# A decoder on one core: the first place in the self attention's work memory, and how that memory is handed over

## The chip, the core and the metric

The kernel runs on one core of a Trainium2 chip. The metric is device time in microseconds (us) for one execution, as a median over runs. The engines are PE (TensorE; PEld is its weight load), DVE (VectorE), ACT (ScalarE), POOL (GpSimd) and SP (SyncE, which issues DMA transfers).

## What is computed

Two decoder layers on `x` of 8 x 256 tokens, 512 wide, all in float32. Each of the six steps adds its result to `x` and normalises:

```python
x = _layernorm(x + _L0_attn_ref(x, ...))    # differential attention
x = _layernorm(x + _L0_xattn_ref(x, ...))   # long convolution
x = _layernorm(x + _L0_ffn_ref(x, ...))     # experts, 2 of 8 for each token
x = _layernorm(x + _L1_attn_ref(x, ...))    # causal self attention, 16 heads of 32
x = _layernorm(x + _L1_xattn_ref(x, ...))   # cross attention
x = _layernorm(x + _L1_ffn_ref(x, ...))     # attention with one routed head of keys and values
```

The change concerns the border between the third step and the fourth, which is

```python
qkv = jnp.einsum('bsd,ed->bse', x, w_qkv).reshape(b, s, 3, H, HD).transpose(2, 0, 3, 1, 4)
q, k, v = qkv[0], qkv[1], qkv[2]
scores = jnp.einsum('bhqd,bhkd->bhqk', q, k) * HD ** (-0.5)
scores = jnp.where(causal, jnp.float32(-1000000000.0), scores)
a = jax.nn.softmax(scores, axis=-1)
ctx = jnp.einsum('bhqk,bhkd->bhqd', a, v).transpose(0, 2, 1, 3).reshape(b, s, d)
return jnp.einsum('bsd,ed->bse', ctx, w_o)
```

## The kernel before

The 2048 tokens are 16 tiles of 128 (`x[0]` to `x[15]`), in four groups of four tiles (`TPG`, `NG`).

**The experts** end in `blocks`. For each block of 128 rows PE makes the result `po_m` (L1164), ACT or DVE copies it to a tile `y_m` (L124, L126), and SP writes that tile to `ys` in DRAM (L1176). These tiles lie in the pool `m_work`. Behind the last block every engine reads a count and branches over spare blocks (L1256, L1263). The first four token tiles are already gathered and normalised during the last blocks, into a part of the weights' tile (the trace calls it `w_l1a`); the other twelve are gathered from `ys` during the self attention, by DMAs that POOL issues (L1279), and added up on DVE (L1287).

**The self attention** is one of three uses of `causal_attention` (L1316): `"a"` is the differential attention, `"s"` the self attention, `"r"` the routed one. It opens a pool of work memory, `{name}_work` (L1337), and pools for PSUM. Then it makes `neg`, `terms` and `take` in the work pool, and goes through units, each a set of four heads of one batch of 256 tokens:

- `maxima` (L1370): scores on PE (`ps_q`, L1378), copied by ACT to `rows` (L1387), masked on POOL (L1389), maxima on DVE (L1398);
- `weights` (L1430): transposed scores on PE (`ps_k`, L1441, L1450), exponentials on ACT (`pT`, L1458), mask and sums on POOL (L1459, L1469);
- `products` (L1471): values and sums on PE (`ps_pv`, L1484, L1495), reciprocal on DVE (L1503).

Projections run between them, in pieces with due times that `fill` and `need` hand out; the order of PE, DVE, ACT and POOL is fixed as it is written (`manual_schedule`). For a group, `prepare` (L1698) makes `qT`, `kT` and `v`, and calls `turned_batches` (L246). That returns steps which turn the tokens, so that the features lie on the partitions: four transposes on PE for each tile (L236) and one copy by ACT into `xT` (L237). One `xT` tile holds one batch, that is two token tiles, and is made when its first step runs; there are three buffers of it. The first projections are `feature_block` (PE `ps_f`, L212, copied by ACT at L1663) for `qT` and `kT`; each reads a whole `xT`. The values are `token_block` (PE `ps_t`, copied by ACT into `v_s`, L1712).

**How memory goes from one pool to the next.** When a pool ends, its bytes are free for the pools opened after it. With `reuse_waits="tile"` the first instruction that writes a tile waits for the instructions and DMAs that used what lay in that tile's own bytes. Without it, the first writes wait for all that used the freed bytes of the pool. Before the change only the work pool of `"r"` has this argument among the three; the pools of the experts that end here (`m_dn`, `m_work`) and the PSUM pools have it too.

Of the kernel before, what the change touches and what calls it, by code (L numbers as in the profile page):

```python
# [17 lines left out]
F32 = mybir.dt.float32  # L18
# [6 lines left out]
P = 128  # L25
B, S, D = 8, 256, 512
# [4 lines left out]
KB = D // P  # L31
# [24 lines left out]
def decoder_kernel(ctx: ExitStack, tc: tile.TileContext, a: dict, out: bass.AP):  # L56
# [175 lines left out]
    def turned(pools, dst, src, tag="mm"):  # L232

        pt = pools.tile([P, KB, P], F32, tag=tag, name="pt")
        for k in range(KB):
            nc.tensor.transpose(pt[:, k, :], src[:, k * P : (k + 1) * P], ident)  # L236
        nc.scalar.copy(dst, pt)  # L237

    class Batches(list):

        def __getitem__(self, at):
            rows, k, tokens = at
            b = tokens.start // S
            return list.__getitem__(self, b)[rows, k, tokens.start - b * S : tokens.stop - b * S]

    def turned_batches(work, pools, g):  # L246

        xT = Batches()

        def step(ti):  # L250
            if ti % 2 == 0:
                xT.append(work.tile([P, KB, S], F32, tag="xT", name="xT", bufs=3))
            dst = list.__getitem__(xT, ti // 2)
            turned(pools, dst[:, :, ti % 2 * P : (ti % 2 + 1) * P], x[g * TPG + ti])

        return [xT], [(0, [(TR, lambda ti=ti: step(ti))]) for ti in range(TPG)]
# [39 lines left out]
    def diff_attention(xh, ch):  # L296
# [213 lines left out]
        def finish(work, pools, t0, yT, at):  # L510
# [71 lines left out]
            return cost  # L582

        causal_attention("a", prepare, finish, 8, gather)
        st0.close()

# [729 lines left out]
    def causal_attention(name, prepare, finish, upb=KB, gather=None):  # L1316
# [17 lines left out]
        }  # L1334
        with ExitStack() as st:
            work = st.enter_context(
                tc.tile_pool(name=f"{name}_work", bufs=2, **({"reuse_waits": "tile"} if name == "r" else {}))  # L1337
            )
            ps_sc = st.enter_context(tc.tile_pool(name=f"{name}_sc", bufs=1, space=PSUM, reuse_waits="tile"))
            ps_pv = st.enter_context(tc.tile_pool(name=f"{name}_pv", bufs=1, space=PSUM, reuse_waits="tile"))  # L1340
# [9 lines left out]

            neg, terms = [], []
            for i in range(2):
                neg.append(work.tile([P, 3, 4, upb], F32, tag=f"neg{i}", name="neg", bufs=1))
# [333 lines left out]
    def self_attention(w, wqkv, homes, arrive):  # L1689
# [8 lines left out]
        def prepare(work, pools, g, at, here):  # L1698
            qT = work.tile([P, KB, GT], F32, tag="qT", name="qT")
            kT = work.tile([P, KB, GT], F32, tag="kT", name="kT")  # L1700
            v = work.tile([P, TPG, D], F32, tag="v", name="v_s")
            xT, turns = turned_batches(work, pools, g)

            def arriving(t, slot, place):
# [47 lines left out]
        def finish(work, pools, t0, yT, at):  # L1752
# [3 lines left out]
            return 2 * KB * MM  # L1756

        causal_attention("s", prepare, finish)


# [204 lines left out]
    def routed_attention(wqkv, wg):  # L1965
# [347 lines left out]
        def finish(work, pools, t0, yT, at):  # L2313
# [10 lines left out]
            return 2 * TR  # L2324

        causal_attention("r", prepare, finish)

    masks, clear_slots, load_experts, load_gu_last, router, blocks, combine, wide = experts(rt)
# [114 lines left out]
```

## Time and profile before

| | |
|---|---|
| median of the runs | 2052.21 us (2049.88 to 2056.38, 3 runs) |
| profiled execution | 2062.48 us, its span 2060.7 us |
| mean granted TensorE clock | 0.983 of full speed |
| experts, last blocks (1000 to 1050 us) | PE busy 50.00 us of 50.00 |
| border (1074 to 1080 us) | PE busy 3.46 us of 6.00, granted clock 0.81 |
| self attention (1120 to 1200 us) | PE busy 79.51 us of 80.00 |
| self attention (1200 to 1300 us) | PE busy 97.25 us of 100.00 |
| routed attention, end (1990 to 2040 us) | PE busy 35.50 us of 50.00, DVE 41.68, clock 0.83 |

All times in a profile count from the start of its span. In a row such as `PE L212 MATMUL ps_f<-xT,w_l1a`, the engine is followed by the source line, the operation and "written tile <- read tiles"; line numbers are those of the kernel before. `PEq`, `ACTq` and the like are the engine's own instruction queue, as apart from its data path. A matmul's end is modelled, so its busy time is approximate.

### The profile page before, as it was taken

The numbers are of one execution on the slowest core, as the hardware profiler recorded it, in microseconds if no ns is written. First come the engines' busy times: TensorE is split into PE (matmuls) and PEld (weight loads), VectorE is DVE, ScalarE is ACT, GpSimd is POOL, SyncE is SP. The second block draws the span as 40 slices with busy tenths as digits, with TensorE's granted clock in tenths as the row PEclk, the third lists the DMA queues.
The fourth block names the chain that finished last, engine by engine and source line by source line (L and its number), as shares of the span: only waits on it lengthen the run. The fifth ranks groups of instructions, "written<-read, shape, count | busy, mean of one in ns | idle before, by whom it ended". The sixth has DMA issues, their size and how long they took to land. (4 is left out here: it accounts for less than half of the span.)

```text
span 2060.7 us, 46451 instructions
## 1 busy us (share of the span) xinstructions
PE 1921.8 (93%) x20142; PEld 1141.9 (55%) x20142; DVE 1253.7 (61%) x1933; ACT 620.1 (30%) x793; POOL 858.0 (42%) x952
## 2 busy tenths in 40 slices
PE   8979999889998998999999999998999999988885
PEld 5545555444443445666555555544888887454443
DVE  4677878758888976122234757456344544437987
ACT  4555555520010003211114434432101011245552
POOL 3687777846556823000014645333100010216763
PEclk9999999989999999999999999999999999999997
DMA  6899953315115125213232212002101000260000
GB/s 230 311 386 380 383 168 84 94 52 212 31 46 184 52 98 188 77 65 129 80 110 84 84 34 83 2 2 81 49 16 41 21 21 1 90 191 15 25 24 32
DMA packets 138044, 219.24 MB, mean 106 GB/s; under 512 B 27440, under 2 KB 52144, under 8 KB 137840
## 3 DMA queue, kind: packets, MB, share of 16 engines
q1 hardware_dynamic: 131376, 195.93, 27.9%
q0 software_dynamic: 6464, 20.32, 2.9%
q8 instruction: 161, 2.64, 0.5%
q14 instruction: 43, 0.35, 0.1%
HBM read 104.42 MB, written 123.34 MB: 111 GB/s over the span
## 5 line engine op out<-in xcount | busy, mean ns | idle before, releaser
L1503 DVE RECIPROCAL rsum<-ps_pv 128x256 f32<-128x256 f32 x128 | 224.5, 1754 | 215.6 <-PE ps_pv L1495 215.4
L182 PE MATMUL ps_y<-kv,wt 128*128 128x512 f32 x640 | 280.0, 596 | 5.2 <-POOL kv L625 2.7
L1398 DVE TENSOR_REDUCE neg<-rows 128x12 f32<-128x1536 f32 x128 | 223.0, 1742 | 53.3 <-POOL rows L1389 53.2
L1458 ACT ACTIVATE pT<-ps_k 128x1536 f32<-128x1536 f32 x128 | 185.7, 1451 | 225.4 <-PE ps_k L1450 218.4
L1459 POOL TENSOR_SCALAR_AFFINE_SELECT pT<-pT 128x1024 f32<-128x1024 f32 x128 | 141.3, 1104 | 217.4 <-ACT pT L1458 217.2
L1387 ACT COPY rows<-ps_q 128x1536 f32<-128x1536 f32 x128 | 184.2, 1439 | 151.0 <-PE ps_q L1378 96.0
L1389 POOL TENSOR_SCALAR_AFFINE_SELECT rows<-rows 128x1024 f32<-128x1024 f32 x128 | 142.3, 1112 | 183.8 <-ACT rows L1387 183.1
L182 PEld LDWEIGHTS ps_y<-kv,wt 128*128 128x128 f32 x640 | 120.8, 191 | 156.3 <-issue 137.7
L1469 POOL TENSOR_TENSOR pT<-pT 128x512 f32<-128x512 f32 x112 | 147.1, 1313 | 9.3
L212 PE MATMUL ps_f<-xT,w_l1a 128*32 128x256 f32 x2048 | 123.4, 385 | 5.5 <-ACT xT L237 4.1
L1164 PE MATMUL po_m<-dn,hT 128*128 (+1 forms) x216 | 100.8, 603 | 4.0 <-issue 2.3
L148 POOL TENSOR_SCALAR rstd<-bn_mv 128x1 f32<-128x1 f32 x80 | 15.8, 198 | 212.5 <-DVE bn_mv L156 206.4
L1143 DVE TENSOR_TENSOR h_b<-h_b,pg 128x352 f32<-128x352 f32 x36 | 18.6, 516 | 124.0 <-ACT h_b L1142 124.0
L1495 PE MATMUL ps_pv<-pT,ones_v 128*32 128x256 f32 (+1 forms) x1152 | 87.1, 381 | 5.2 <-POOL pT L1469 5.1
L212 PEld LDWEIGHTS ps_f<-xT,w_l1a 128*32 128x32 f32 x2048 | 62.9, 111 | 51.2 <-issue 9.0
L663 DVE TENSOR_REDUCE yc<-z 128x64 f32<-128x512 f32 x128 | 86.1, 673 | 5.7 <-issue 5.2
L1279 POOL DMA_INDIRECT y<-ys,slots x4 | 4.0, 1007 | 204.4 <-PE pu L182 203.8
L1378 PEld LDWEIGHTS ps_q<-kT,qT 32*128 32x128 f32 x1536 | 49.5, 188 | 50.5 <-issue 18.1
L182 PE MATMUL pg<-gu,xT_b 128*128 x216 | 72.1, 470 | 3.6 <-ACT xT_b L237 3.6
L1378 PEld LDWEIGHTS ps_q<-kz,qT 32*128 32x128 f32 x1536 | 49.2, 188 | 47.2 <-ACT pT L1458 33.7
L1378 PE MATMUL ps_q<-kz,qT 32*128 32x128 f32 x1536 | 61.5, 289 | 14.3 <-ACT pT L1458 11.6
L1378 PE MATMUL ps_q<-kT,qT 32*128 32x128 f32 x1536 | 61.9, 290 | 12.7 <-ACT pT L1458 8.7
(411 smaller groups left out, 3694.2 us busy)
## 6 DMA issues: line engine op xcount, KB each, us to landing
xs<-zero SPq DMA_DIRECT2D x8, 4352.0 KB
ys<-zero SPq DMA_DIRECT2D x8, 4352.0 KB
filters<-in_L_xattn_k SPq DMA_DIRECT2D x4, 2560.0 KB
first_h<-xs SPq DMA_DIRECT2D x36, 256.0 KB
ys<-y_m SPq DMA_DIRECT2D x36, 256.0 KB
gu<-in_L_ffn_gate_up_proj SPq DMA_DIRECT2D x3, 2816.0 KB
wt<-filters SPq DMA_DIRECT2D x32, 256.0 KB
sorted_x<-zero SPq DMA_DIRECT2D x1, 5120.0 KB
```

The source lines that it names most:

```text
L182: nc.tensor.matmul(ps, lhsT=lhsT(k), rhs=rhs(k), start=(k == 0), stop=(k == n - 1))
L212: nc.tensor.matmul(ps[cs], lhsT=lhsT[:, cs], rhs=rhs, start=start, stop=stop)
L1164: nc.tensor.matmul(po, lhsT=hT[:m, i, :], rhs=dn[i][:m, bass.ds(e, 1), :], start=(i == 0), stop=(i == len(FCH) - 1),)
L1378: nc.tensor.matmul(block[:, s, j, :], lhsT=q(rows, c, b * S + i * P, P), rhs=k(rows, c, b * S + keys * P, P), start=True, stop=True,)
L1387: nc.scalar.copy(d.rearrange("p j s k -> p s j k"), block)
L1389: nc.gpsimd.affine_select(out=rows, in_=rows, compare_op=ALU.is_ge, fill=-FAR, base=0, pattern=[[0, 8], [-1, P]], channel_multiplier=1,)
L1398: return lambda: nc.vector.tensor_reduce(neg[u // upb % 2][:, :, :, c], d, AX.X, ALU.max, negate=True)
L1458: nc.scalar.activation(p[:, 0:3].rearrange("p j s q -> p s j q"), block, AF.Exp)
L1459: nc.gpsimd.affine_select(out=p[:, 0:2].rearrange("p j s q -> p (j s) q"), in_=p[:, 0:2].rearrange("p j s q -> p (j s) q"), compare_op=ALU ...
L1469: nc.gpsimd.tensor_tensor(p[:, 3], p[:, 1], p[:, 2], ALU.add)
L1495: nc.tensor.matmul(ps[32 * s : 32 * s + 32, 1, j * P :], lhsT=ones_v, rhs=p[:, 1, s, :] if j else first[:, :, s, :], start=(j == 0), stop= ...
L1503: nc.vector.reciprocal(r, ps[:, 1, :])
```

## The change

Three edits:

- In `causal_attention("s", ...)` the first tile made in the work pool is now an `xT` tile, made ahead of `neg`, `terms` and `take`, and left in a list `placed`.
- `turned_batches` takes that tile for its first batch, and makes its own for all later ones.
- The work pools of `"s"` and `"r"` are both handed over with `reuse_waits="tile"`; before, only that of `"r"` was.

```diff
+    placed = []
+
     def turned_batches(work, pools, g):
...
             if ti % 2 == 0:
-                xT.append(work.tile([P, KB, S], F32, tag="xT", name="xT", bufs=3))
+                xT.append(
+                    placed.pop()
+                    if placed
+                    else work.tile([P, KB, S], F32, tag="xT", name="xT", bufs=3)
+                )
...
-                tc.tile_pool(name=f"{name}_work", bufs=2, **({"reuse_waits": "tile"} if name == "r" else {}))
+                tc.tile_pool(name=f"{name}_work", bufs=2, **({} if name == "a" else {"reuse_waits": "tile"}))
...
+            if name == "s":
+                placed.append(work.tile([P, KB, S], F32, tag="xT", name="xT", bufs=3))
             neg, terms = [], []
```

In the built program the instructions of each engine stand in the same order before and after. What differs are the conditions some of them wait for:

| instruction (line before) | conditions before | after |
|---|---|---|
| ACT, first copy into `xT` (L237) | PE, 14 DMA counters, DVE, POOL, ACT | PE |
| PE, first `ps_f` (L212) | ACT, 15 DMA counters, DVE | ACT |
| DVE, `terms` (L1357) | PE, ACT, DVE, 6 DMA counters | an earlier PE instruction |
| POOL, first `rows` (L1389) | ACT, 8 DMA counters, DVE | ACT, 1 earlier DMA |
| POOL, four of the gathers (L1279) | data, earlier gathers | 1 or 2 DMA counters more |
| ACT, first `kT` (L1663) | PE | PE, earlier ACT and DVE instructions |
| PE, first `ps_q` (L1378) | ACT | ACT, DVE |
| ACT, first `v_s` (L1712) | PE | PE, 10 DMA counters |
| ACT, one `pT` (L1458) | PE | PE, 1 DMA counter |
| DVE, one `less` (L1412) | DVE | DVE, an earlier PE instruction |
| ACT, one copy in the cross attention (L1819) | PE, DVE | PE, DVE, 2 DMA counters |

## The prediction

> **What bounds the kernel now.** I read the page first: the span, the busy shares, and the granted clock.
>
> ```profile
> span 2060.7 us, 46451 instructions
> PE 1921.8 (93%) x20142; PEld 1141.9 (55%) x20142; DVE 1253.7 (61%) x1933; ACT 620.1 (30%) x793; POOL 858.0 (42%) x952
> PEclk9999999989999999999999999999999999999997
> ```
>
> PE is busy for 93% of the span, so there are few places where a wait can be taken out. Only one of them concerns this change: the start of the self attention. The chain of work that ended last, in order of time, shows it (start, length, what):
>
> ```profile
> 1074.11 2.00 DMA ys<-y_m
> 1076.11 0.02 issue
> 1076.13 0.04 ACTq L237
> 1076.17 0.04 issue
> 1076.21 1.08 ACT xT L237 x2
> 1077.30 0.04 issue
> 1077.34 5.39 PE ps_f L212 x64
> ```
>
> The last rows of the experts are written to DRAM, and only when that write has landed does ACT copy the first turned tokens; PE's first projection waits for the copy. The copies read the transposes and nothing of that write. Then the timeline (start, length, engine, line, operation, and in brackets the idle time before it with what ended it); the last line is a later stretch for comparison:
>
> ```profile
> 1073.50 0.59 ACT L124 COPY y_m<-po_m 128x512 f32<-128x512 f32 x1 [2.98 <-PE po_m L1164]
> 1073.72 1.08 PE L236 MATMUL pt<-ident,w_l1a 128*128 128x128 f32 x8 [0.30 <-PEq L1263]
> ...
> 1077.34 5.35 PE L212 MATMUL ps_f<-xT,w_l1a 128*32 128x256 f32 x64 [2.54 <-ACT xT L237]
> ...
> 1192.68 4.09 PE L212 MATMUL ps_f<-xT,w_l1a 128*32 128x256 f32 x72
> ```
>
> The transposes were done at 1074.80, and PE then stood idle for 2.54 us. What follows is slow too: 64 matmuls in 5.35 us, where 72 of the same kind later take 4.09 (64 by that rate: 3.64). Busy time by stretch tells why (stretch, length, PE, PEld, DVE, ACT, POOL busy with their instructions, granted clock, DMA share, GB/s):
>
> ```profile
> 1074.30:1077.71 3.41, 0.87 (x13) 0.55 (x15) 0.33 (x3) 1.07 (x2) 0.00 (x0) 1.00 0.35 129
> 1077.71:1081.13 3.42, 3.42 (x40) 1.70 (x33) 0.00 (x0) 0.38 (x1) 0.00 (x0) 0.50 1.01 379
> ...
> 1753.55:1756.97 3.42, 3.42 (x28) 2.86 (x27) 2.28 (x8) 2.33 (x5) 0.80 (x3) 1.00 0.00 0
> ...
> 1797.93:1801.34 3.41, 1.78 (x33) 1.17 (x34) 0.87 (x2) 0.58 (x1) 2.34 (x3) 1.00 0.85 308
> 1801.34:1804.75 3.41, 3.41 (x22) 1.28 (x17) 0.00 (x0) 1.44 (x1) 0.17 (x1) 0.50 0.34 105
> 1893.50:1896.91 3.41, 1.81 (x40) 1.18 (x40) 3.38 (x5) 2.34 (x2) 2.09 (x2) 1.00 0.00 0
> 1896.91:1900.33 3.42, 2.96 (x52) 1.32 (x56) 3.21 (x8) 1.44 (x2) 2.20 (x4) 1.00 0.23 81
> ```
>
> Every change of the granted clock lies on one grid of 3.41 us. A stretch of that grid in which PE is busy 0.87 or 1.78 us is followed by one at clock 0.50; after 1.81 us the clock stays at 1.00. So the wait costs twice: once as idle time, and once as a half-speed stretch behind it, in which PE was busy throughout.
>
> **The change part by part.** In the built program the order of instructions on all five engines is unchanged and no DMA is added or moved. Only waits differ, so the parts are waits.
>
> *The first copies and the first projection.* ACT's copy of xT loses 17 wait conditions and keeps the one on PE; PE's first `ps_f` loses 16 and keeps the one on ACT. When can the copies start? ACT ends its last `y_m` copy at 1073.50 + 0.59 = 1074.09 and the branch behind it by 1074.2 (ACT's own queue at L1263). Tile 0's four transposes end between 1073.72 + 0.54 (half of the eight) and 1073.72 + 0.66 (a lone group of four at 1095.59 takes 0.66). I take 1074.4 as the start, a little above both. The two copies together take 1.08, as in the chain, and tile 1's transposes, done at 1074.80, are there before the second copy wants them. End 1075.48; with 0.04 to PE (the chain's "issue") and a little for a semaphore, `ps_f` starts at 1075.55 and not at 1077.34: 1.8 us. Bounds: a start at 1074.26 gives 1077.34 − 1075.38 = 1.96; a start only after all eight transposes (1074.80 + 0.13) gives 1077.34 − 1076.05 = 1.29.
>
> *The half-speed stretch.* PE's idle time before `ps_f` becomes 0.30 + (1075.55 − 1074.80) = 1.05 us. However the grid falls, a stretch of 3.41 us then holds at least 2.36 us of PE work, well over the 1.81 after which the clock stayed up. The half-speed stretch therefore goes, and with it half of 3.41 = 1.71 us (by the rates above: 5.35 − 3.64 = 1.71, the same). Bounds: 0, if that stretch is not on this run's grid or stays for a reason not seen, and 1.71. I take 1.71, because it stands in the row.
>
> [...]
>
> *The waits that appear elsewhere.* The places of the tiles are new, so waits come up where a tile now lies on old bytes. ACT's first copy of `v_s` gets ten DMA conditions. They are among those that `xT` had, and all were met at 1076.11; the value projection (`ps_t`) that feeds this copy starts at 1102.96 in the chain. Queued behind that copy on ACT is `rows` L1387, for which POOL, then DVE, then PE would wait; the cover is some 27 us before and 23 after, so nothing. The first gathers on POOL get two writes to `ys` to wait for; they ran at 1093.60, and about 1090 after, 14 us behind the landing; behind them stands POOL's next `rows` select. `kT`, the first `ps_q`, `terms`, `less`, the first POOL `rows`, one `pT` and `u2` of the cross attention get one to three conditions each, on instructions that ended by 1076. Extra conditions cost 0.02 to 0.05 us each on a queue (the queue rows of L1263); ten of them before `v_s` are at most 0.5 us on ACT, which stands idle for 2 to 3 us around there. I put all of it at 0, bounds 0 and 0.5.
>
> *Does the gain reach the end?* After 1077 the waits list of all engines names DMA as the releaser of DVE's L1287 (4.9 us in total, gathers that POOL issues in step with the units), and of L2146 and L2158 (5.0 us, rows sorted on the chip just before). All are started by earlier work, so they move along. From 1080 to 1425 PE is busy in 95 to 99% of the time. What was PE's chain stays PE's chain, 3.5 us earlier.
>
> Sum: −1.8 − 1.71 + 0 = −3.5 us. The profiled execution took 2062.48 us (span 2060.7 and 1.8 around it), which becomes 2059.0 with a span of 2057.2. The median of the runs is 2052.21, 10.3 below the profiled one, so the gain is carried over as microseconds: 2048.7.
>
> **The rivals.**
>
> [...]
>
> *C: the change does not do what it says,* or another wait takes the place: the copies still end at about 1077. For it: the last write still takes its 2.00 us, and ten conditions of it still stand in ACT's queue. Against it: they stand 18 instructions later, at `v_s`. 2052.2.
>
> *D: slower, by the clock grid.* All later work moves against the grid. In the profile, seven stretches after 1082 had PE busy 52 to 58% and stayed at full clock (1893.50 is one; the others begin at 1429.29, 1432.70, 1941.29, 1992.49, 2006.14 and 2040.27). If only the wait goes, they move by 1.8 us, half a grid step, and may fall under. Each one that tips costs up to 1.71; from two (3.4) on, this eats the gain of 1.8. With four: 4 × 1.71 − 1.8 = +5.0: 2057.2. For it: unchanged runs lie between 2049.88 and 2056.38, nearly four such steps apart. Against it: the full gain of 3.5 is one whole grid step (3.41), so the later work comes to lie nearly as before; and after 1985 the chain runs through DVE for long parts, where PE's clock costs less.
>
> *E: the same, in the other direction:* two half-speed stretches fewer later on (the trace has them at 1801, 1835, 1999, 2020 and 2027): 3.5 + 3.4 = 6.9 less, 2045.3.
>
> **How the numbers follow.** Forecast A (2048.7) 0.50, B 0.14, C 0.12, D 0.10, E 0.14. A measurement of this kernel can tell about 0.3% from no change, 6.2 us: under 2046.0 is faster, over 2058.4 slower. The runs before lie from 2.3 below their median to 4.2 above it, and a median of a few runs moves by 2 to 3. So a quarter of A's weight (0.13) may come out under 2046, and E all of it: faster 0.27. Slower is D's upper part and what I have not seen, 0.08. Same 0.65. For the range, A with that scatter is 2046 to 2052; to leave out no more than 2 in 10 it takes in C and the nearer parts of D and E: 2043.5 to 2055.
>
> **What would show it.** Right: the chain at the start of the self attention has no `ys<-y_m` in it any more; ACT's two `xT` copies start near 1074.4 and no longer behind a DMA; PE's idle time before the first `ps_f` is about 0.8 us; 64 `ps_f` take 3.6 to 3.7 us and the clock there is 1.00; the first `ps_q` starts about 3.5 us earlier, and that distance still stands at the end of the self attention. Wrong: `ps_f` starts early but still takes over 5 us (B); a wait on a DMA in front of `v_s`, the gathers or `rows` (C); the distance shrinks in the last 250 us with more stretches at 0.50 (D).

## The result, and the profile after

| | before | after |
|---|---|---|
| median of 21 runs each, us | 2052.21 (2047.49 to 2056.95) | 2047.24 (2042.50 to 2052.47) |
| ratio after / before | | 0.998, 95% interval 0.9972 to 0.9989 |
| profiled execution, its span, us | 2060.7 | 2045.5 |

In this comparison the changed kernel is 0.2% faster: 5.0 us by the medians, 4.1 (2.3 to 5.7) by the ratio. That is less than the 0.3% at which the prediction began to call it faster. Two later comparisons of the same two kernels (medians of before 2059.43 and 2058.56 us) gave 0.9994 (0.9980 to 1.0008) and 0.9995 (0.9981 to 1.0009), neither of them clear of no change by itself. The three, weighted by the width of their intervals, give about 0.9986 (0.9980 to 0.9993), 2.8 us.

The page of the profile after begins so:

```profile
span 2045.5 us, 46438 instructions
PE 1915.1 (94%) x20142; PEld 1139.1 (56%) x20142; DVE 1253.4 (61%) x1933; ACT 620.6 (30%) x793; POOL 857.2 (42%) x952
PEclk9999999999999999999999999999999999999998
```

The span is 15.2 us shorter, but that is not what the change gives. The first transposes of the border began at 1064.84 and not at 1073.72: 8.9 us are gone ahead of everything that the change touches. From there to the end of the self attention (its last `ps_o`) the traces differ by 6.0 us, and behind it by 0.3. Not all of the 6.0 is the change either: three more traces of the changed kernel, further below, take 1.4 to 3.4 us longer for that part. What the change does is read from the border. Its chain of waits (start, length, what):

```profile
1064.84 0.64 PE pt L236 x4
1065.48 0.02 issue
1065.50 1.08 ACT xT L237 x2
1066.58 0.04 issue
1066.63 3.71 PE ps_f L212 x64
```

The write `ys<-y_m` is no longer in it. ACT's copies follow the transposes of their own tile, and PE follows the copies. In the timeline (start, length, engine, line, operation, idle time before it and what ended it), with the first copy of the values as the last line:

```profile
1064.84 1.08 PE L236 MATMUL pt<-ident,w_l1a 128*128 128x128 f32 x8 [0.30 <-PEq L1269]
1065.23 0.33 SPq L1182 DMA_DIRECT2D ys<-y_m  x1
1065.50 1.07 ACT L237 COPY xT<-pt 128x512 f32<-128x512 f32 x2 [0.30 <-PE pt L236]
1066.63 3.66 PE L212 MATMUL ps_f<-xT,w_l1a 128*32 128x256 f32 x64 [0.71 <-ACT xT L237]
...
1095.00 0.59 ACT L1720 COPY v_s<-ps_t 128x512 f32<-128x512 f32 x1 [0.41 <-PE ps_t L212]
```

The copies start only 0.27 us after SP has begun to issue the write that they used to wait for, so they cannot have waited for its landing, which came 2.0 us after its issue. PE stands idle for 0.71 us and not for 2.54, and 64 `ps_f` take 3.66 us and not 5.35. The `v_s` copy, which took over ten DMA conditions, waits for PE alone. By stretch of the clock's grid (stretch, length, PE, PEld, DVE, ACT, POOL busy, granted clock, DMA share, GB/s):

```profile
1062.60:1066.01 3.41, 3.02 (x13) 1.41 (x11) 0.33 (x3) 1.09 (x3) 0.00 (x0) 1.00 0.19 70
1066.01:1069.43 3.42, 2.80 (x52) 1.72 (x56) 0.00 (x0) 0.95 (x3) 0.00 (x0) 1.00 0.62 195
1069.43:1072.84 3.41, 2.86 (x63) 1.71 (x59) 0.00 (x0) 1.37 (x2) 0.00 (x0) 1.00 0.91 338
```

No stretch holds less than 2.80 us of PE work, and none is at half speed.

### The profile page after: what moved, and what is told of

Same layout as the page of the kernel before. It is cut to its first block, busy times and chain, and to the rows that moved or that the text cites. A ratio compares the mean times of both kernels' runs of the same rounds, so it can differ in the third digit from the quotient of the medians.

```text
span 2045.5 us, 46438 instructions
## 1 busy us (share of the span) xinstructions
PE 1915.1 (94%) x20142; PEld 1139.1 (56%) x20142; DVE 1253.4 (61%) x1933; ACT 620.6 (30%) x793; POOL 857.2 (42%) x952
## 5 line engine op out<-in xcount | busy, mean ns | idle before, releaser
L212 PE MATMUL ps_f<-xT,w_l1a 128*32 128x256 f32 x2048 | 120.3, 381 | 3.4 <-ACT xT L237 2.2
L212 PEld LDWEIGHTS ps_f<-xT,w_l1a 128*32 128x32 f32 x2048 | 61.9, 110 | 47.0 <-issue 5.6
L1449 PE MATMUL ps_k<-qT,kT 32*128 32x256 f32 (+1 forms) x1024 | 69.9, 360 | 5.3 <-ACT rows L1395 3.1
```

The source lines that it names most:

```text
L212: nc.tensor.matmul(ps[cs], lhsT=lhsT[:, cs], rhs=rhs, start=start, stop=stop)
L1449: nc.tensor.matmul(block[:, s, at, :], lhsT=k(rows, c, b * S + j * P, P), rhs=q(rows, c, b * S + j * P, P * (2 - j)), start=True, stop=False,)
```

## The experiments

**Each half of the change alone.** The first kernel (place_only) has the new first tile but hands the pool over as before; the second (tiles_only) has the hand-over by tile but no new first tile. Both diffs are against the changed kernel.

```diff
-  **({} if name == "a" else {"reuse_waits": "tile"})
+  **({"reuse_waits": "tile"} if name == "r" else {})
```

```diff
-  if name == "s":
-      placed.append(work.tile([P, KB, S], F32, tag="xT", name="xT", bufs=3))
```

> The kernel before with the first place for xT, but the work pool still handed over as a whole. Read at the border, from the start of PE's first two groups of token transposes (pt) to the first projection (ps_f) and to the first scores (ps_q): before 3.62 and 9.47 us, with the change 1.79 and 6.00. Theory (the place alone does nothing, because without the handover by tile every first write waits for all of the old memory): 3.6, and 9.5 if the half-speed stretch falls there, else down to 7.8. Rival (the place is what frees the copies): 1.8 and 6.0.

> The kernel before with the handover by tile, but xT made after neg, terms and take as before. In the built program the first copy into xT then still has six of the transfers of y_m among its conditions, since xT lies on their bytes. Theory (both edits are needed): ACT's copy starts when the last write of ys has landed, 3.6 us from pt to ps_f, and 9.5 (or down to 7.8) to ps_q. Rival (the handover alone brings the gain): 1.8 and 6.0. A third way: xT waits for an earlier write of ys only, something between, 2 to 3 us.

In one run each, beside one of the kernel before at 2062.30 us, they took 2058.93 and 2068.58. Single runs scatter by more than that, so the border decides: from the first transposes to `ps_f` 3.62 us in both, as before, and to `ps_q` 9.28 and 9.22. The chain of waits of the hand-over alone, and the stretches of the clock's grid around it:

```profile
1080.88 2.00 DMA ys<-y_m
1082.88 0.02 issue
1082.90 0.04 ACTq L237
1082.94 0.04 issue
1082.98 1.08 ACT xT L237 x2
1084.07 0.04 issue
1084.11 5.14 PE ps_f L212 x64
```

```profile
1080.22:1083.63 3.41, 1.08 (x8) 0.84 (x8) 0.33 (x3) 1.23 (x3) 0.00 (x0) 1.00 0.21 79
1083.63:1087.04 3.41, 2.93 (x28) 1.38 (x32) 0.00 (x0) 0.43 (x1) 0.00 (x0) 0.50 0.95 317
```

Without the new first tile, the bytes of `xT` are those of old `y_m` tiles, and a wait by tile still means six DMA conditions of their writes. With the new place but a hand-over as a whole, the conditions are those of before, word for word. Either half alone gives nothing; the gain needs both.

**The wait kept, PE kept busy in it.** Two kernels are the kernel before with work on PE between the first transposes and the wait: 20 transposes whose results nobody reads (fill_turns), and 5 products of 512 columns likewise (fill_products). If half speed comes from PE's idle time, either takes it away and leaves the wait. If it does, but transposes are not work that keeps the clock up, only the products do. If the landing writes slow the matmuls, neither does.

```diff
             turned(pools, dst[:, :, ti % 2 * P : (ti % 2 + 1) * P], x[g * TPG + ti])
+            if g == 0 and ti == 1:
+                spare = pools.tile([P, KB, P], F32, tag="mm", name="pt_z")
+                for i in range(20):
+                    nc.tensor.transpose(spare[:, i % KB, :], ident, ident)
```

```diff
             turned(pools, dst[:, :, ti % 2 * P : (ti % 2 + 1) * P], x[g * TPG + ti])
+            if g == 0 and ti == 1:
+                spare = pools.tile([P, D], F32, tag="mm", name="ps_z")
+                for i in range(5):
+                    nc.tensor.matmul(spare, lhsT=ident, rhs=x[0], start=True, stop=True)
```

> The kernel before, with the wait left in, and 20 transposes of the identity added on PE behind the first two groups of transposes; their result is read by nobody. At the rate of the eight (about 0.12 us each) they take 2.3 us of the 2.54 that PE waits there. Theory (the wait costs a second time through the clock, and transposes keep the clock up): pt to ps_f stays 3.6, no stretch at clock 0.50 behind it, 64 ps_f in 3.66 and not 5.35 us, pt to ps_q 7.8. Rival (transposes do not count as PE work for the clock): clock 0.50 behind it, 64 ps_f in about 5.3, ps_q at 9.5. Second rival (the slow projections come from the DMA traffic beside them and not from PE's idle time): also 5.3 and 9.5.

> The same with 5 ordinary products of 128x512 (about 0.45 us each, 2.2 us) in place of the 20 transposes, their result unread. Theory and the rival on transposes both say: pt to ps_f 3.6, clock 1.00, 64 ps_f in 3.66 us, ps_q at 7.8. Only the rival on DMA traffic says 5.3 and 9.5.

They took 2058.29 and 2059.12 us in one run each. The timeline of PE with the transposes, and the stretches of the grid:

```profile
1075.01 1.08 PE L236 MATMUL pt<-ident,w_l1a 128*128 128x128 f32 x8 [0.30 <-PEq L1267]
1075.92 2.35 PE L258 MATMUL pt_z<-ident 128*128 128x128 f32 x20
1078.62 3.66 PE L212 MATMUL ps_f<-xT,w_l1a 128*32 128x256 f32 x64 [0.36 <-ACT xT L237]
```

```profile
1073.44:1076.86 3.42, 3.12 (x20) 2.05 (x20) 0.00 (x0) 0.58 (x1) 0.00 (x0) 1.00 0.20 75
1076.86:1080.27 3.41, 3.05 (x45) 2.21 (x47) 0.33 (x3) 1.07 (x2) 0.00 (x0) 1.00 0.66 222
1080.27:1083.68 3.41, 2.91 (x66) 1.70 (x58) 0.00 (x0) 0.77 (x2) 0.00 (x0) 1.00 0.66 243
```

`ps_f` still starts 3.62 us after the first transposes (1078.62 − 1075.01 = 3.61), so the wait is whole, but the 64 matmuls take 3.66 us and `ps_q` comes after 7.78 us. That is what the theory says, but this trace alone does not show that the added work kept the clock up. Without it the stretch from 1076.86 would have held only the `ps_f` from 1078.62 on, 1.65 us or 48%, and stretches with such a share went either way (of those with 48 to 52%, 12 of 35 were followed by half speed, counted further below). The fill of another wait, in the last experiment, settles it. The writes are not what slows the matmuls: the DMA engines are 66% busy here at clock 1.00, and 91%, also at 1.00, in the last stretch shown of after. With the products PE's timeline reads:

```profile
1076.20 4.46 PE L258 MATMUL ps_z<-w_l1a,ident 128*128 128x512 f32 x10
1080.59 3.66 PE L212 MATMUL ps_f<-xT,w_l1a 128*32 128x256 f32 x64
```

The 64 `ps_f` take 3.66 us here too, as at clock 1.00 with the transposes, but five products are ten matmul records of some 0.45 us. They outlast the wait, `ps_f` starts after 5.30 us, and `ps_q` after 9.47. I had sized them too large. Nor does the run tell the theories apart: on its grid (stretches from 1074.25 and 1077.66) PE would have been busy 53 and 63% even without the products and with `ps_f` at its 3.62 us, and at such shares the clock mostly stayed up (17 of 151 stretches with 52 to 60% were followed by half speed, and 2 of 7746 with more, counted further below).

**The two kernels again, and four more waits filled.** At four other places PE waits in the same way: before `ps_n` in the differential attention (3.38 us in the trace of after), at the start (2.87) and once in the middle (2.71) of the long convolution, and in front of the routed attention (1.79). The last kernel of this group (filled) is the changed kernel with unread transposes there, into tiles that are about to be written; in the convolution's `turn` the number is handed on to `transpose`, which makes them ahead of its own.

```diff
+    def keep_busy(out, n):
+        for i in range(n):
+            nc.tensor.transpose(out[:, i % out.shape[1], :], ident, ident)
...
                 ps = pools.tile([P, 2, P], F32, tag="mm", name="ps_n")
+                if name == "a" and n == 0:
+                    keep_busy(ps, 24)
...
-                turn(t)
+                turn(t, 18 if t == 2 * EARLY else 0)
...
                     ps = psum.tile([P, B, NHEAD, NHEAD], F32, tag="y", name="ps_y")
+                    if (h, lb) == (NH // 2, KB - 1):
+                        keep_busy(ps.rearrange("p b i j -> p (b i j)").rearrange("p (k c) -> p k c", k=KB), 16)
...
                 for ti in range(TPG):
+                    if g == 0 and ti == TPG - 1:
+                        keep_busy(pt[:, ti:, :], 12)
```

> The kernel before once more, for a second trace. Theory: pt to ps_f 3.6 us again (it is set by the landing of a write), and the half-speed stretch behind it wherever the 3.41 us grid lets PE's idle time fall into one stretch, which by the idle times (0.30 and 2.54 us) and the bound of about 1.8 busy us is nearly always: pt to ps_q 9.2 to 9.5. If the grid alone decided (rival: chance), ps_q would as often come at 7.8. From ps_f to the end of the self attention's projections, 348.8 us in the first trace and 344.7 with the change: if the 2.5 us of that which lie behind the half-speed stretch are noise of one trace, this trace comes out anywhere between; if they belong to the change, it is 348 to 349 again.

> The changed kernel once more. Theory: pt to ps_f 1.8, to ps_q 6.0, no stretch at clock 0.50 at the border, whatever the grid. Against the kernel before 0.9977 to 0.9983 (3.5 to 4.7 us). From ps_f to the end of the self attention 344.7 if the 2.5 us behind the half-speed stretch belong to the change, about 347 if they are noise of one trace.

> The changed kernel with transposes of the identity, unread, put in four other waits of PE, all outside the self attention: 24 before the first ps_n of the differential attention (PE waits 3.4 us for DVE there), 18 before the long convolution's first transposes (2.9 us, for DVE), 16 in its middle (2.7 us, for POOL), 12 before the last keys of the routed attention are turned (1.8 us, for DVE). Theory (a wait of PE of over about 1.6 us costs a half-speed stretch on top, up to 1.71 us, and filling it with transposes takes that away): no stretch at 0.50 behind these four, up to 4 x 1.7 = 6.8 us less than the changed kernel, 3 to 6 where PE is not the bound right behind: ratio to the kernel before 0.9950 to 0.9970. Rival (those stretches are hidden behind DVE or POOL, or the added work delays PE by as much): the same as the changed kernel, 0.998.

The changed kernel came out at 0.9994, where 0.9977 to 0.9983 was expected. The filled kernel, expected at 0.9950 to 0.9970, was slower: 2062.07 us against 2059.43, ratio 1.0016 (1.0004 to 1.0029). In its trace only the first and the last fill stand at their place. The two in the convolution lie outside the order that is written by hand, and the scheduler moved them: 18 transposes ran at 435 to 440 us, among other work and well ahead of the wait, and 16 at 614 to 620. The border itself also got worse, by something unforeseen:

```profile
1078.36 1.06 PE L237 MATMUL pt<-ident,w_l1a 128*128 128x128 f32 x8 [1.67 <-PEq L1277]
1080.15 5.22 PE L213 MATMUL ps_f<-xT,w_l1a 128*32 128x256 f32 x64 [0.72 <-ACT xT L238]
```

```profile
L1277 PEldq COMPARE_BRANCH  x1: 3368/3368/3368, 1074.7 to 1074.7; - x1
```

```profile
1076.54:1079.95 3.41, 1.22 (x9) 0.86 (x8) 0.33 (x3) 1.51 (x3) 0.00 (x0) 1.00 0.24 84
1079.95:1083.36 3.41, 3.21 (x32) 1.59 (x36) 0.00 (x0) 0.15 (x1) 0.00 (x0) 0.50 0.80 220
```

PE's branch over the spare blocks (second fence: shortest, median and longest time in ns) took 3.37 us; it took 0.38 in every other trace of this study. PE therefore idled 1.37 us longer ahead of the transposes, the stretch held 1.22 us of work, and a half-speed stretch followed in spite of the change: `ps_f` after 1.79 us, `ps_q` after 7.57. That is 2.9 us of the loss (1.37 and 7.57 − 6.00). How the rest divides over the moved fills is not settled.

The repeat of the kernel before brought a trace without the half-speed stretch:

```profile
1074.75:1078.16 3.41, 1.38 (x28) 0.86 (x32) 0.33 (x3) 1.07 (x2) 0.00 (x0) 1.00 0.56 190
1078.16:1081.58 3.42, 2.92 (x64) 1.75 (x60) 0.00 (x0) 0.77 (x2) 0.00 (x0) 1.00 0.84 303
```

The wait is there (`ps_f` after 3.63 us), yet PE's work around it fell on the grid so that the stretch held 1.38 us, 40%, and the clock stayed up. The 64 `ps_f` took 3.66 us there, with the same writes landing beside them (DMA engines 84% busy at clock 1.00; 101% at 0.50 in the first trace of before, with 5.35 us for the 64), so it is the clock and not the writes that makes them slow.

**How often the half-speed stretch comes.** So both kernels were traced twice more.

> The kernel before, a further trace. In nine traces so far every grid stretch with PE busy under 40% was followed by clock 0.50 (61 of 61), between 40 and 56% only some, above 60% 2 of some 330. By that the wait at the border (2.54 us idle, 0.30 before the transposes) makes a half-speed stretch in about two of three traces: pt to ps_q 9.2 to 9.5 with it, 7.8 without, and pt to ps_f 3.6 in any case. Rival (it is there always, as the prediction had it): 9.2 to 9.5 in all.

> The kernel before, one more trace, with the same theories: pt to ps_f 3.6 in any case; pt to ps_q 9.2 to 9.5 with a half-speed stretch at the border (two of three traces), 7.8 without; the rival has 9.2 to 9.5 in all.

> The changed kernel again, for a trace and for the ratio. pt to ps_f 1.8 and to ps_q 6.0, without a half-speed stretch at the border unless PE's branch in front of it takes longer than the usual 0.3 us. Gain to be expected by 1.8 + two thirds of 1.7 = 3.0 us: 0.9985; the first comparison gave 0.998, the second 0.9994. From ps_f to the end of the self attention about 347, as in all traces but the first one of this kernel.

> The changed kernel, one more trace: pt to ps_f 1.8 and to ps_q 6.0, no half-speed stretch at the border unless the branch before it takes longer than 0.3 us; about 347 us from ps_f to the end of the self attention.

The border in every trace of a kernel without added work, in us from its first transposes:

| trace | ACT's copies | `ps_f` | `ps_q` | `ps_f` to `ps_q` | half-speed stretch | end of self attention |
|---|---|---|---|---|---|---|
| before | 2.49 | 3.62 | 9.47 | 5.85 | yes | 353.0 |
| before_again | 2.50 | 3.63 | 7.79 | 4.16 | no | 350.8 |
| before_c | 2.50 | 3.62 | 9.09 | 5.47 | yes | 352.3 |
| before_d | 2.50 | 3.62 | 9.30 | 5.68 | yes | 352.2 |
| place_only | 2.50 | 3.62 | 9.28 | 5.66 | yes | 352.9 |
| tiles_only | 2.50 | 3.62 | 9.22 | 5.60 | yes | 354.2 |
| after | 0.66 | 1.79 | 6.00 | 4.21 | no | 347.0 |
| after_again | 0.67 | 1.79 | 6.01 | 4.21 | no | 349.4 |
| after_c | 0.67 | 1.79 | 6.01 | 4.21 | no | 348.5 |
| after_d | 0.67 | 1.79 | 6.01 | 4.21 | no | 350.5 |

The wait is worth 1.83 us in every trace. The half-speed stretch came in five of the six traces with the wait and in none of the four without. Where it came it cost 1.26 to 1.64 us (`ps_f` to `ps_q`, less 4.21). The 1.64 is the first trace of before, where it began with PE's work under way; in the other four it began 0.3 to 0.7 us ahead of `ps_f`, on idle time, and `ps_f` started after 3.62 us all the same. Over the six it is 1.19 us on average.

Before and after part by part, over four traces each: the self attention ends 352.10 and 348.85 us after the first transposes, and the span ends 632.1 and 632.7 us after that.

**One fill alone.** The last kernel (filled_one) is the changed kernel with only the fill ahead of `ps_n`, which stood in the order written by hand.

```diff
                 ps = pools.tile([P, 2, P], F32, tag="mm", name="ps_n")
+                if name == "a" and n == 0:
+                    keep_busy(ps, 24)
```

> The changed kernel with one of the four fills of the run before: 24 unread transposes on PE ahead of the first ps_n of the differential attention, the fill that stood in the right place. Two questions. First, whether the same double cost (a wait plus a half-speed stretch behind it) goes at another wait: in nine traces without this fill the first ps_pv came 10.5 to 11.8 us after the first ps_n (mean 11.0), in the one with it 9.06. If the fill does it, 9.1 to 9.3 us again and no half-speed stretch between 46 and 55 us; if that was one trace's luck, 10.5 or more. The time would then be about 2 us under the changed kernel's: a ratio to the kernel before near 0.9976 (0.9986 from the three comparisons, and 0.0010 less), with an interval that can't tell it from the changed kernel's own. Second, PE's branch at the border, 376 to 385 ns in eleven traces and 3368 in the run with four fills: if the long branch comes from any added PE instruction ahead of it, it is over 3 us here too and ps_q comes about 7.6 us after the first transposes; if it comes from the other three fills or from where they put the code, 0.38 us and 6.0.

```profile
44.24 2.78 PE L251 MATMUL ps_n<-ident 128*128 128x128 f32 x24
47.78 0.30 PE L1435 MATMUL ps_n<-ident_b,terms 128*32 128x128 bf16 x8 [0.77 <-DVE terms L1422]
...
56.85 0.83 PE L1499 MATMUL ps_pv<-pT,v 128*32 128x256 f32 x16
...
1075.47 1.08 PE L236 MATMUL pt<-ident,w_l1a 128*128 128x128 f32 x8 [0.30 <-PEq L1274]
1077.26 3.66 PE L212 MATMUL ps_f<-xT,w_l1a 128*32 128x256 f32 x64 [0.71 <-ACT xT L237]
```

The stretch of the grid that holds most of the fill:

```profile
44.62:48.03 3.41, 2.65 (x31) 2.30 (x29) 3.20 (x8) 1.19 (x2) 1.09 (x1) 1.00 0.52 206
```

Of its 2.65 us, 2.40 are the unread transposes (44.62 to 47.02). Without them 0.25 us, 7%, would be left, and in each of the twelve traces without this fill one or two half-speed stretches came at this place. So the unread transposes are what keeps the clock up.

The wait is there (2.78 us of it filled, 0.77 left), no half-speed stretch follows (the clock is 1.00 from 43 to 57 us), and the first `ps_pv` comes 9.06 us after the first real `ps_n`, to the hundredth what the other trace with this fill had, where unfilled ones had 10.5 to 11.8. PE's branch took 376 ns and the border is as in after, so an added instruction ahead of the branch is not by itself what makes it long. The time was 2054.85 us (2048.07 to 2057.55) against 2059.58, ratio 0.9972 (0.9955 to 0.9989). That is the lowest ratio of the study, but it overlaps those of the changed kernel: that the fill saves 1.4 to 2.8 us at its place, against the unfilled traces, is shown; that the whole becomes faster than with the change alone is not.

## Why the prediction was right, step by step

*The first copies and the first projection.* Right, in mechanism and in size. The copies started 0.66 us after the first transposes where the prediction put 0.7, `ps_f` after 1.79 us where it put 1.83, and PE's idle time is 0.71 us. The term was −1.8, and it is −1.83 in every pair of traces. tiles_only and place_only show that it takes both edits.

*The half-speed stretch.* Right as a mechanism, over-sized, and its reason was too sharp. The term was −1.71, with 0 as its other bound "if that stretch is not on this run's grid". That bound happened, in one trace of six, and where the stretch came it cost 1.26 to 1.64. On average the term is −1.19. The error lay in the sentence that a stretch with 1.78 us of PE work is followed by half speed while "after 1.81 us the clock stays": two rows stood for a threshold. A stretch that the prediction itself lists among those that stayed at full clock, the one at 1941.29, already spoke against it: it holds 1.78 us too.

```profile
1941.29:1944.70 3.41, 1.78 (x48) 1.26 (x44) 3.38 (x3) 1.45 (x1) 2.74 (x5) 1.00 0.00 0
1944.70:1948.12 3.42, 2.50 (x54) 1.45 (x54) 3.42 (x4) 1.44 (x1) 2.88 (x3) 1.00 0.38 138
```

Over the stretches at full clock in 14 traces, without the first 12 and the last 25 us of each:

| PE's share of the stretch | followed by half speed |
|---|---|
| under 40% | 85 of 85 |
| 40 to 48% | 43 of 57 |
| 48 to 52% | 12 of 35 |
| 52 to 60% | 17 of 151 |
| over 60% | 2 of 7746 |

There is a mixed zone from 40 to 60%, and both of those rows (52 and 53%) lie in it. The claim that after the change a stretch holds at least 2.36 us "however the grid falls" held in the four traces of after, but it rested on an idle time of 0.30 us ahead of the transposes; with the 1.67 us that the long branch left there in the filled kernel it did not hold.

*Transposes and the clock.* The prediction counts the transposes of the border as PE work: its bound of 2.36 us leaves out only the idle time before and behind them. The trace of before agrees with that. The busy time of L236, transposes alone, in the stretches from 1753.55 on (stretch, length, PE and PEld busy, granted clock, DMA share, GB/s):

```profile
1753.55:1756.97 3.42, 2.97 (x26) 2.86 (x27) 1.00 0.00 0
1756.97:1760.38 3.41, 2.48 (x22) 2.14 (x21) 1.00 0.00 0
1760.38:1763.79 3.41, 1.99 (x19) 1.82 (x18) 1.00 0.00 0
```

PE is busy throughout the three, and without these transposes the first two would hold 0.45 and 0.93 us; the clock stays at 1.00. The runs bear it out. In filled_one the stretch from 44.62 holds 78% of PE work with its unread transposes and 7% without them, and the clock stayed at 1.00. If transposes are left out of PE's busy time, 325 of the stretches in those 14 traces come out under 40%, and only 112 of them were followed by half speed; counted as work, all 85 were.

*The waits that appear elsewhere.* Right at 0. The `v_s` copy waits for PE alone with its ten more conditions, and the four traces of after agree within 0.01 us from the first transposes to `ps_q`, with all the conditions in place.

*Does the gain reach the end?* Right, as far as the scatter lets it be seen. Against 3.0 us at `ps_q` (1.83 + 1.19), 3.25 us are there at the end of the self attention over four traces each (352.10 − 348.85); but the four traces of after alone lie 3.4 us apart there. The part behind it is 0.5 us longer on average, well within the scatter of that part from trace to trace (630.1 to 633.9).

*The sum* was −3.5; by the terms as measured it is −3.0, and the three comparisons together give −2.8 (−1.4 to −4.1). The 5.0 of the medians holds some 2 us of scatter, and the two later comparisons gave 1.2 and 1.0 us, so how near the first one came to the forecast is partly luck. The range, 2043.5 to 2055, also holds the unchanged 2052.21: the time alone could not have told the forecast from no effect, and it is the border in the traces that does.

*The rivals.* B (only the wait goes, 1.8 us) falls with filled_one and with the border in the four traces of after, though in one of the six traces with the wait, the wait was all that there was to lose. C (it does not do what it says) is what either edit alone does, and not the change. D and E (half-speed stretches gained or lost later, by the grid) show as noise and not as an effect of the change: behind the self attention the four traces of before have 7, 6, 5 and 4 such stretches ahead of the span's last, those of after 8, 6, 6 and 4. In the traces with 4 or 5 of them that part takes 630.2 to 630.7 us, in those with 6 to 8 it takes 632.4 to 633.9. So they go with a good part of the scatter, which leaves single runs of one kernel up to 14 us apart (2053.27 to 2067.26 for before in the second comparison) and hides an effect of 3 to 4.

## What to carry to other kernels

Where a pool of memory is opened on bytes that others have just left, ask for each early writer in the chain which old bytes its tile lies on: here the wait by tile helped only when the first tile was also put where nothing was still in flight (`ps_f` after 1.79 us, and after 3.62 with either edit alone). A wait of 2.5 us on PE was paid twice here, as idle time (1.83 us of it went) and in five traces of six again as a half-speed stretch (1.26 to 1.64 us); if such a wait cannot go, unread transposes in it can take away the second payment, as they did ahead of `ps_n` (first `ps_pv` after 9.06 us, 10.5 to 11.8 without), provided that their place is fixed (two of the four fills moved) and they end before the wait does (the five products did not, and `ps_f` came after 5.30 us). And a threshold read from two neighbouring rows is a guess: look for rows of the same share that went the other way, and count the stretches on both sides, in several traces, before a term is built on it.

## What the runs showed of the hardware

*The mixed zone of the clock* in the table above: from 40 to 60% of PE work, 72 of 243 stretches at full clock were followed by half speed, under 40% all 85, over 60% 2 of 7746.

*A branch whose time jumps.* PE's COMPARE_BRANCH at the border took 376 to 385 ns in 13 traces and 3368 in one kernel, that with four fills. With the first of them alone (filled_one) it took 376. Whether one of the other three makes it long was not tried, and the cause stays open.
